# Four layers on 128 small graphs: sums over a graph in any division of the array, s spread as a diagonal, a chunk's sums and its H B⁻¹ Hᵀ in one four-quarter operation

## The chip, the cores and the metric

The kernel runs on one core of a Trainium2 chip. The metric is the device time of one execution in microseconds, the median of three runs. The profile is of one further execution of the same program.

## The reference, cut to what matters

There are 128 graphs of 64 nodes with 512 features each. Four residual layers follow each other, each ending in a layer norm over the features. `A` is the graph's own 64 x 64 matrix `adj`.

```python
# layer 0: additive attention
s = (x @ w) @ a                              # one number per node
A0 = tanh((s_i + s_j) / 8) * 8
A0 = where(A0 >= 0, A0, 0.1 * A0)
A0 = exp(A0) * A;  A0 /= A0.sum(-1);  A0 *= A.sum(-1)
x = layernorm(x + A0 @ x @ w)
# layer 1: attention, adj * exp(q k'), rows divided by their sum
weight = A * exp(q @ k.T);  x = layernorm(x + (weight / weight.sum(-1)) @ v)
# layer 2: a gate, softmax over the nodes of the graph
L = softmax(inv_scale * mask * sum((A @ (k * mask)) * q, -1)) * v
x = layernorm(x + L)
# layer 3: two hypergraph convolutions around a layer norm
H = (A != 0);  D = H @ A[0];  B = H.sum(rows)
conv(h, W) = D^-1 H B^-1 H' (h @ W') + b
x = layernorm(x + conv(layernorm(relu(conv(x, W1))), W2))
```

## The kernel before, in words

Two graphs lie side by side on the 128 partitions: a tile is 64 nodes of one graph on partitions 0 to 63 and 64 of another on 64 to 127. Two tiles make a group (`GT = 2`), so there are 32 groups (`NG`), and two groups make a chunk of four tiles (`CT = 4`), so there are 16 chunks. `run(g)` records all steps of one group, `prepare_chunk(c)` what is computed from `adj` alone for a chunk. The big products with the 512-wide weights are seven-product (Strassen-like) schemes over halves, `seven_products`, which stream their weight pieces (`ring`) from memory. All data are fp32; on TensorE every fp32 product is two passes in the trace (a transpose is one), so a line of the timeline counts twice the products of the code. A 128-row pass with a 128-column load is called whole below.

A product within one graph needs 64 rows and 64 columns of the array only. The kernel marks each TensorE operation with a mode: `whole` (128 x 128), `columns` (128 x 64, in `scores`), or `quarters` (64 x 64). In the quarters mode a product takes a quarter by the partitions of its operands (rows) and of its output (columns). `gathered` uses all four quarters in turn; `over_graph`, the sums and `emit_g` in `prepare_chunk`, and `emit_s` use the two quarters on the diagonal only. In the trace `bank<-kept,x`, `bank<-kept,h` and `bank<-e,x` are `gathered`, `bank<-k,k 128*64` is `scores`, `bank<-e,same` is `over_graph`, `bank<-ident,col 64*64` is `emit_s`, `bank<-ones,adj` and `bank<-w,kept` are the chunk's sums, `bank<-kept,kept` is the chunk's H B⁻¹ Hᵀ, `bank<-ones,e` is layer 1's row sum (f in the code), and `bank<-k,e 64*64` is the product with v after it (po).

Nothing of this is issued as recorded. `Order` is a planner: every operation is added with an engine, an assumed cost, its reads and writes, and a key. `Order.run` then plays the whole program once and takes, on each engine, the ready operation with the lowest key whose buffers are free. On TensorE it charges 145 ns (`TURN`) for a change of mode and prefers an operation of the mode it is in, within `NEAR` (0.5) of the lowest key while in the whole mode and within `FAR` (6.0) otherwise. The order found is pinned on every engine; each engine then issues strictly in it, and everything goes through one recording helper, which is why all lines of the profile carry one line number. Four PSUM banks (kind `bank`) and two pairs (`chx`, `chz`) hold the results of TensorE; `e` is a pool of seven 128 x 2 x 64 buffers.

The parts the change touches, by name: in `prepare_chunk`, `hA` (adj != 0), `be` (one over its row sums), `bh` (hA times be, on GpSimd), `w` (adj's first row with ones beside it), `sums` and `emit_g`; in `run`, `emit_s`, which spreads the column s over the graph, the addition of s to it and the tanh after it; the two uses of `over_graph`, one for layer 0's `e`, one for layer 2's `pr`; and `f`, `ps_f`, `po` of layer 1. Two copies of a chunk's matrix are loaded: `adj` (one transfer) and `turned` (four transfers), in which the tiles' halves are placed so that a four-quarter product meets the right graph.

Of the kernel before, what the change touches and what calls it, by code (L numbers as in the profile page):

```python
# [16 lines left out]
P = 128  # L17
# [37 lines left out]
class Op:  # L55
    __slots__ = ("engine", "cost", "emit", "key", "missing", "users", "takes", "touches", "start", "bytes", "step", "mode", "port", "behind", "group")


class Order:
    LATENCY = {"PE": 220, "DVE": 70, "ACT": 60, "POOL": 60, "SP": 2200}  # L60
    BYTES_PER_NS = 300
    UNDERWAY = 8
    TURN = 145

# [7 lines left out]
    def add(self, engine, cost, reads, writes, emit, urgent=0.0, size=0, mode=None, port=False):  # L72
        o = Op()
        o.engine, o.cost, o.emit, o.key, o.step = engine, cost, emit, self.key - urgent, self.key
        o.start, o.mode, o.port, o.behind, o.group = None, mode, port, None, self.group
        o.users, o.takes, o.touches, o.bytes = [], [], [], size
# [41 lines left out]
    def run(self):  # L118
# [11 lines left out]
        while len(done) < len(self.ops):  # L130
# [4 lines left out]
            for e, heap in ready.items():  # L135
                while free_at[e] <= now:
                    skipped, held, found = [], set(), None
                    while heap:
# [7 lines left out]
                        if item[2].port and port_free > now:  # L146
                            skipped.append(item)
                        elif all(k not in held and len(self.slots[k]) >= c for k, c in need.items()):
                            fits = e != "PE" or item[2].mode == mode
                            if found is None or fits:  # L150
                                if found:
                                    skipped.append(found)
                                found, takes = item, wants
                            else:
                                skipped.append(item)
                            if fits or found[0] < 0:
                                break
                        else:
                            held.update(need)
                            skipped.append(item)  # L160
# [6 lines left out]
                    if e == "PE":  # L167
                        turn, mode = self.TURN if found.mode != mode else 0, found.mode
                    found.start = now
# [60 lines left out]
def kernel(  # L230
# [29 lines left out]
    def sb(name, *shape):  # L260
        return sbuf.tile([P, *shape], FP, name=name)
# [65 lines left out]
    for rows, cols in halves:  # L327
        nc.vector.memset(same[rows, cols], 1.0)

    eye = sb("eye", N)  # L330
    nc.vector.tensor_add(eye, ident[:, :N], ident[:, N:])
# [98 lines left out]
    pe(w_pe(P, KC), [u0], [ps_u0], lambda: emit_u0(ps_u0))  # L430
    act(D, [ps_u0], [u0_b], lambda: nc.scalar.copy(u0_b.t, ps_u0.t))

# [201 lines left out]
    def per_tile(v):  # L634
        return v[:, :, None].to_broadcast([P, CT, N])
# [10 lines left out]
    def prepare_chunk(c):  # L646
        order.key = BASE[GC * c] - 3.0 if c else 0.5
        adj = adjs[c]
        m = mask_c.t[:, ts(c, CT)]
        hA, bh, am = (Buf("kept") for _ in range(3))  # L650
        be = Buf("col")

        dve(W, [adj], [hA, turn], lambda: nc.vector.tensor_scalar(hA.t, adj.t, 0.0, None, ALU.not_equal))
        dve(W, [hA], [be], lambda: nc.vector.tensor_reduce(be.t[:, :CT], hA.t, AX.X, ALU.add))
        dve(CT, [be], [be], lambda: nc.vector.tensor_scalar(be.t[:, :CT], be.t[:, :CT], 1.0, None, ALU.max))
        dve(CT, [be], [be], lambda: nc.vector.reciprocal(be.t[:, :CT], be.t[:, :CT]))

        w = Buf("w")
        act(CT, [adj], [w], lambda: nc.scalar.copy(w.t[:, :, 0:1], adj.t[:, :, 0:1]))

        ps = Buf("bank")

        def sums():
            for left, right, n, at in ((adj, lambda t: ones, 1, 0), (hA, lambda t: w.t[:, t], 2, 1)):
                for t in range(CT):
                    for rows, _ in halves:
                        nc.tensor.matmul(ps.t[rows, 4 * t + at : 4 * t + at + n], left.t[rows, t], right(t)[rows],
                                         start=True, stop=True)

        pe(900, [adj, hA, w], [ps], sums, mode="quarters")  # L670
        radj, n_edges, dn = Buf("col"), Buf("col"), Buf("col")
        g1, dc, dh = Buf("col"), Buf("col"), Buf("col")

        def out(i):
            return ps.t[:, : 4 * CT].rearrange("p (t k) -> p t k", k=4)[:, :, i]

        dve(CT, [ps], [radj], lambda: nc.vector.tensor_copy(radj.t[:, :CT], out(0)), NOW)
        dve(CT, [ps], [dn], lambda: nc.vector.tensor_copy(dn.t[:, :CT], out(1)), NOW)
        dve(CT, [ps], [n_edges], lambda: nc.vector.tensor_copy(n_edges.t[:, :CT], out(2)), NOW)

        dve(CT, [dn], [dc], lambda: nc.vector.tensor_scalar(dc.t[:, :CT], dn.t[:, :CT], TINY, None, ALU.max))
        dve(CT, [dc], [dc], lambda: nc.vector.reciprocal(dc.t[:, :CT], dc.t[:, :CT]))
        dve(CT, [dn, dc], [dc], lambda: nc.vector.scalar_tensor_tensor(
            dc.t[:, :CT], dn.t[:, :CT], 0.0, dc.t[:, :CT], ALU.is_gt, ALU.mult))
        dve(CT, [dc], [dh], lambda: nc.vector.tensor_scalar(dh.t[:, :CT], dc.t[:, :CT], 0.5, None, ALU.mult))

        dve(CT, [dc, n_edges], [g1], lambda: nc.vector.tensor_mul(g1.t[:, :CT], dc.t[:, :CT], n_edges.t[:, :CT]))

        pool(W, [hA, be], [bh], lambda: nc.gpsimd.tensor_mul(bh.t, hA.t, per_tile(be.t[:, :CT])))

        ps_g, gm = Buf("bank"), Buf("kept")

        def emit_g():
            for t in range(CT):
                for rows, _ in halves:
                    nc.tensor.matmul(ps_g.t[rows, ts(t, N)], hA.t[rows, t], bh.t[rows, t], start=True, stop=True)

        pe(500, [hA, bh], [ps_g, gm], emit_g, mode="quarters")
        act(W, [ps_g], [gm], lambda: nc.scalar.copy(flat(gm.t), ps_g.t[:, :W]), NOW)

# [7 lines left out]
        dve(W, [am, mr], [am], lambda: nc.vector.tensor_mul(am.t, am.t, mr.t))  # L708
        prepared[c] = adj, turned_adjs[c], gm, am, radj, g1, dc, dh

# [208 lines left out]
    def over_graph(v, ps):  # L919


        def emit():
            for rows, _ in halves:
                nc.tensor.matmul(ps.t[rows, : GT * N], same[rows, rows], flat(v.t)[rows], start=True, stop=True)

        pe(w_pe(P), [v], [ps], emit, mode="quarters")

# [27 lines left out]
    def run(g):  # L955
# [11 lines left out]

        s = Buf("col", GT)
        for t in range(GT):
            row_dot([xt[[2 * t, 2 * t + 1]], u0_b], s[t], lambda t=t: xt.t[:, t, :], lambda: u0_b.t)  # L970
        ps_s = Buf("bank")

        def emit_s():
            for t in range(GT):
                for rows, cols in halves:
                    nc.tensor.matmul(tiles(ps_s)[rows, t, :], s.t[rows, t : t + 1].to_broadcast([N, N]), ident[rows, cols],
                                     start=True, stop=True)

        pe(300, [s], [ps_s], emit_s, mode="quarters")
        e = Buf("e")  # L980
        dve(GT * N, [ps_s, s], [e], lambda: nc.vector.tensor_add(
            e.t, tiles(ps_s), s.t[:, :GT][:, :, None].to_broadcast([P, GT, N])), NOW)
        act(GT * N, [e], [e], lambda: nc.scalar.activation(e.t, e.t, AF.Tanh, scale=0.125))
        dve(GT * N, [e], [e], lambda: nc.vector.scalar_tensor_tensor(e.t, e.t, 0.1, e.t, ALU.mult, ALU.max))
# [31 lines left out]
        dve(GT * N, [e1, turned], [e1], lambda: nc.vector.tensor_mul(e1.t, e1.t, turned.t[:, own]))  # L1016
        step(6)

        f = Buf("col", GT)
        ps_f = [Buf("bank") for _ in range(GT)]  # L1020

        def quadrants(out, left, right):
            for h, (cols, _) in enumerate(halves):
                for t, (rows, _) in enumerate(halves):
                    nc.tensor.matmul(out(t)[cols], left(h)[rows], right(h)[rows], start=True, stop=True)

        pe(150, [e1], ps_f, lambda: quadrants(lambda t: ps_f[t].t[:, 0:1], lambda h: e1.t[:, h, :], lambda h: ones), mode="quarters")
        po = [Buf("bank") for _ in range(GT)]
        for t in range(GT):
            dve(1, [ps_f[t]], [f[t]], lambda t=t: nc.vector.reciprocal(f.t[:, t : t + 1], ps_f[t].t[:, 0:1]), NOW)  # L1030
        pe(w_pe(D), [e1, v], po, lambda: quadrants(
            lambda t: po[t].t, lambda h: e1.t[:, h, :], lambda h: v.t[:, ts(h, D)]), mode="quarters")
        for t in range(GT):
            dve(D + 40, [po[t], f[t], xt[[2 * t, 2 * t + 1]]], [xt[[2 * t, 2 * t + 1]]],
                lambda t=t: nc.vector.scalar_tensor_tensor(xt.t[:, t, :], po[t].t, f.t[:, t : t + 1], xt.t[:, t, :],
                                                   ALU.mult, ALU.add), NOW)
# [119 lines left out]
    for o in order.run():  # L1156
        for b in o.takes:
            b.t = kinds[b.kind][b.slot]
        if o.behind:
            behind.append(names[o.behind])  # L1160
        o.emit()
        if o.port and o.engine == "DVE":
# [42 lines left out]
```

## Time and profile before

| | |
|---|---|
| median of three runs | 2191.93 us (2191.6 to 2192.64) |
| the profiled execution, its own time | 2194.68 us |
| its span, first to last instruction | 2192.8 us |
| PE busy | 2166.0 us, 21587 passes |
| PEld (weight loads) busy | 1744.5 us |
| DVE busy | 1562.4 us (71%) |
| ACT busy | 823.2 us (38%) |
| POOL busy | 385.7 us (18%) |
| mean granted TensorE clock | 0.997 |
| DMA | 476.44 MB, mean 217 GB/s |

A group of passes in the timeline has a start, a length that reaches to the end of its last pass, and a count. Passes overlap in the array, so what a group costs its engine is the distance from its start to the start of the next group, not its length.

### The profile page before, as it was taken

The page shows a single profiled execution, that of the slowest core. Times are in us where ns is not written, and L with a number is a line of the kernel's source. Part 1 is how long each engine was busy: PE and PEld are TensorE (multiplying, and loading weights), DVE is VectorE, ACT ScalarE, POOL GpSimd, SP SyncE. Part 2 cuts the span into 40 slices and gives each one's busy share as a digit, 9 for nine tenths or more (in the row PEclk, how much of TensorE's full clock was granted, in tenths as well). Part 3 has the DMA queues.
Part 4 walks back from the last instruction along what each step waited for, and adds up shares of the span by engine and source line. Part 5 has one row for each costly group of instructions (what it writes and reads, how often), then busy time and mean ns, then how long its engine had stood idle before and what let it go on. Part 6 is the DMA issues. An engine that isn't in the chain of part 4 may idle for free.

```text
span 2192.8 us, 52900 instructions
## 1 busy us (share of the span) xinstructions
PE 2166.0 (99%) x21587; PEld 1744.5 (80%) x21587; DVE 1562.4 (71%) x4044; ACT 823.2 (38%) x1700; POOL 385.7 (18%) x399
## 2 busy tenths in 40 slices
PE   8999999999999999999999999999999999999998
PEld 4887787888888878888878888788888788888866
DVE  5787766677777777777777777777777777776675
ACT  1344342443334333333433343333343333343433
POOL 1112221121111211112121111211112211122111
PEclk9999999999999999999999999999999999999999
DMA  9766567676665666666576656766556766666475
GB/s 304 255 233 217 192 218 263 202 243 222 211 203 203 207 235 215 209 203 222 197 245 205 210 202 205 228 214 230 197 202 207 240 208 210 203 196 228 154 244 209
DMA packets 174306, 476.44 MB, mean 217 GB/s; under 512 B 35760, under 2 KB 45296, under 8 KB 174064
## 3 DMA queue, kind: packets, MB, share of 16 engines
q1 hardware_dynamic: 174064, 473.05, 64.6%
q8 instruction: 171, 2.80, 0.5%
q14 instruction: 71, 0.58, 0.1%
HBM read 443.33 MB, written 29.66 MB: 216 GB/s over the span
## 4 chain that ended last, share of the span: by engine, by line
PE 97%; DMA 1%; DVE 1%; issue 0%; ACT 0%; SPq 0%; DVEq 0%; ACTq 0%
PE bank L1134 40%; PE chx L1134 35%; PE chz L1134 23%; DMA x<-in_x_dram 0%; DMA out_dram<-x 0%; DMA k<-in_wk_dram 0%; DVE col L1134 0%; DVE x L1134 0%; ACT k L1134 0%; DVE h L1134 0%; ACT x L1134 0%; DVE e L1134 0%; DVE k L1134 0%; SPq L1134 0%; DVE m L1134 0%
## 5 line engine op out<-in xcount | busy, mean ns | idle before, releaser
L1134 PE MATMUL chx<-ring,k 128*128 128x256 f32 (+1 forms) x1664 | 481.2, 418 | 2.6 <-issue 2.0
L1134 PE MATMUL bank<-ring,k 128*128 128x256 f32 (+1 forms) x1536 | 424.5, 417 | 0.3 <-ACT k L1134 0.3
L1134 PEld LDWEIGHTS chx<-ring,k 128*128 128x128 f32 x1664 | 310.2, 191 | 91.7 <-issue 52.7
L1134 POOL TENSOR_TENSOR col<-col,mhalf 128x2 f32<-128x2 f32 (+1 forms) x161 | 111.5, 693 | 1481.1 <-DVE col L1134 910.7
L1134 PEld LDWEIGHTS bank<-ring,k 128*128 128x128 f32 x1536 | 286.2, 191 | 87.4 <-issue 52.0
L1134 ACT COPY k<-bank 128x512 f32<-128x512 f32 (+1 forms) x448 | 226.4, 560 | 343.9 <-PE bank L1134 330.4
L1134 ACT ACTIVATE x<-x,col,col 128x512 f32<-128x512 f32 x256 | 198.2, 811 | 193.1 <-DVE col L1134 185.0
L1134 PE MATMUL chz<-ring,h 128*128 128x256 f32 (+1 forms) x768 | 242.8, 452 | 0.0
L1134 PEld LDWEIGHTS chx<-k,m 128*128 128x128 f32 x1536 | 192.1, 192 | 30.9 <-issue 21.3
L1134 PE MATMUL chx<-k,m 128*128 128x128 f32 x1536 | 203.7, 276 | 0.8 <-DVE h L1134 0.8
L1134 DVE SCALAR_TENSOR_TENSOR x<-chx,col,x 128x256 f32<-128x256 f32 x384 | 173.8, 478 | 42.0 <-PE chx L1134 37.0
L1134 PE MATMUL chz<-ring,k 128*128 128x256 f32 x768 | 201.3, 385 | 0.0
L1134 DVE SCALAR_TENSOR_TENSOR x<-bank,col,x 128x256 f32<-128x256 f32 (+1 forms) x256 | 137.8, 549 | 84.3 <-PE bank L1134 78.7
L1134 PE MATMUL chx<-ring,h 128*128 128x256 f32 (+1 forms) x640 | 181.2, 422 | 0.0
L1134 PEld LDWEIGHTS chz<-ring,h 128*128 128x128 f32 x768 | 141.3, 191 | 48.2 <-issue 34.1
L1134 DVE BATCH_NORM_STATS2 col<-x 128x6 f32<-128x512 f32 x256 | 173.4, 687 | 5.7 <-DVE x L1134 0.5
L1134 PEld LDWEIGHTS chz<-ring,k 128*128 128x128 f32 x768 | 141.9, 191 | 19.6 <-issue 1.4
L1134 PEld LDWEIGHTS chx<-ring,h 128*128 128x128 f32 x640 | 120.6, 191 | 34.5 <-issue 21.0
L1134 DVE SCALAR_TENSOR_TENSOR x<-chz,col,x 128x256 f32<-128x256 f32 x192 | 92.7, 483 | 69.6 <-PE chz L1134 67.1
L1134 ACT ACTIVATE h<-h 128x512 f32<-128x512 f32 x128 | 80.7, 632 | 152.8 <-DVE h L1134 152.3
L1134 PEld LDWEIGHTS chz<-k,m 128*128 128x128 f32 x1024 | 127.0, 192 | 12.3 <-issue 11.9
L1134 PE MATMUL chz<-k,m 128*128 128x128 f32 x1024 | 135.6, 276 | 0.0
(118 smaller groups left out, 2801.5 us busy)
## 6 DMA issues: line engine op xcount, KB each, us to landing
ring<-3a SPq DMA_DIRECT2D x224, 512.0 KB, 4.6
ring<-3b SPq DMA_DIRECT2D x224, 512.0 KB, 4.2
ring<-v SPq DMA_DIRECT2D x189, 512.0 KB, 4.3
ring<-w SPq DMA_DIRECT2D x93, 512.0 KB, 4.5
x<-in_x_dram SPq DMA_DIRECT2D x32, 512.0 KB, 4.5
ring<-v SPq DMA_DIRECT2D x63, 256.0 KB, 3.6
out_dram<-x SPq DMA_DIRECT2D x31, 512.0 KB, 3.3
ring<-w SPq DMA_DIRECT2D x31, 256.0 KB, 4.8
```

Of the source, the lines that this page charges most:

```text
L1134: made = f(*args, **kwargs)
```

## The change

`over_graph` gets the mode `any`: where the planner is in the whole mode the operation is one whole product with the block-diagonal matrix of ones `same`, elsewhere it is two products on the diagonal quarters. The planner decides when it places it. A turn between the two divided modes is now charged at 60 ns, one into or out of the whole mode at 145 ns as before. Layer 0's s is spread by the same `over_graph`: ScalarE multiplies `eye` (two stacked 64 x 64 identities) by s, and the sum over the graph spreads it; the addition of s and the tanh become two activations with a bias, and the factor 1/8 moves into the constant u0. Layer 1's row sums are one whole product of e1 with a two-column matrix `row_of`. The chunk's sums and H B⁻¹ Hᵀ become one operation that reads `turned` and uses all four quarters.

```diff
-    TURN = 145
+    TURN, TURN_DIVIDED = 145, 60
...
-                            fits = e != "PE" or item[2].mode == mode
+                            fits = e != "PE" or item[2].mode in (mode, "any")
...
-                        turn, mode = self.TURN if found.mode != mode else 0, found.mode
+                        if found.mode == "any":
+                            found.mode = "whole" if mode in ("whole", None) else "quarters"
+                            found.args = (found.mode == "whole",)
+                        if found.mode != mode:
+                            turn = self.TURN if "whole" in (found.mode, mode) else self.TURN_DIVIDED
+                        mode = found.mode
...
+    row_of = sb("row_of", GT)
+    nc.vector.memset(row_of, 0.0)
+    for t, (rows, _) in enumerate(halves):
+        nc.vector.memset(row_of[rows, t : t + 1], 1.0)
...
-    act(D, [ps_u0], [u0_b], lambda: nc.scalar.copy(u0_b.t, ps_u0.t))
+    act(D, [ps_u0], [u0_b], lambda: nc.scalar.activation(u0_b.t, ps_u0.t, AF.Identity, scale=0.125))
...
-        dve(W, [adj], [hA, turn], lambda: nc.vector.tensor_scalar(hA.t, adj.t, 0.0, None, ALU.not_equal))
+        dve(W, [turned], [hA, turn], lambda: nc.vector.tensor_scalar(hA.t, turned.t, 0.0, None, ALU.not_equal))
...
-        pe(900, [adj, hA, w], [ps], sums, mode="quarters")
...
-        pe(500, [hA, bh], [ps_g, gm], emit_g, mode="quarters")
-        act(W, [ps_g], [gm], lambda: nc.scalar.copy(flat(gm.t), ps_g.t[:, :W]), NOW)
...
+        ps = [Buf("bank") for _ in range(2)]
+        def quarters_of(n, at, left, right):
+            for g in range(CT // 2):
+                for h, (cols, _) in enumerate(halves):
+                    for t, (rows, _) in enumerate(halves):
+                        nc.tensor.matmul(ps[t].t[cols, at(g) : at(g) + n], left.t[rows, 2 * g + h], right(2 * g + h)[rows],
                                          start=True, stop=True)
+        def emit_g():
+            quarters_of(N, lambda g: N * g, hA, lambda i: bh.t[:, i])
+            quarters_of(1, lambda g: P + 3 * g, turned, lambda i: ones)
+            quarters_of(2, lambda g: P + 3 * g + 1, hA, lambda i: w.t[:, i])
+        pe(720, [turned, hA, bh, w], [*ps, gm], emit_g, mode="quarters")
+        for t in range(2):
+            act(P, [ps[t]], [gm], lambda t=t: nc.scalar.copy(
+                gm.t.rearrange("p (g t) i -> p t g i", t=2)[:, t], ps[t].t[:, :P].rearrange("p (g i) -> p g i", i=N)), NOW)
+            dve(6, [ps[t]], [sums], lambda t=t: nc.vector.tensor_copy(
+                sums.t[:, : 3 * CT].rearrange("p (k g t) -> p t g k", t=2, k=3)[:, t],
+                ps[t].t[:, P : P + 6].rearrange("p (g k) -> p g k", k=3)), NOW)
...
-        def emit():
-            for rows, _ in halves:
+        def emit(whole):
+            for rows in (slice(0, P),) if whole else (rows for rows, _ in halves):
                 nc.tensor.matmul(ps.t[rows, : GT * N], same[rows, rows], flat(v.t)[rows], start=True, stop=True)
-        pe(w_pe(P), [v], [ps], emit, mode="quarters")
+        pe(w_pe(P), [v], [ps], emit, mode="any")
...
-        pe(300, [s], [ps_s], emit_s, mode="quarters")
-        dve(GT * N, [ps_s, s], [e], lambda: nc.vector.tensor_add(
-            e.t, tiles(ps_s), s.t[:, :GT][:, :, None].to_broadcast([P, GT, N])), NOW)
-        act(GT * N, [e], [e], lambda: nc.scalar.activation(e.t, e.t, AF.Tanh, scale=0.125))
+            act(N + 40, [s[t]], [diag[t]], lambda t=t: nc.scalar.activation(diag.t[:, t], eye, AF.Identity, scale=s.t[:, t : t + 1]))
+        over_graph(diag, ps_s)
+        for t in range(GT):
+            act(N + 40, [ps_s, s[t]], [e[t]], lambda t=t: nc.scalar.activation(
+                e.t[:, t], tiles(ps_s)[:, t], AF.Tanh, bias=s.t[:, t : t + 1]), NOW)
...
-        pe(150, [e1], ps_f, lambda: quadrants(lambda t: ps_f[t].t[:, 0:1], lambda h: e1.t[:, h, :], lambda h: ones), mode="quarters")
+        pe(110, [e1], [ps_f], lambda: nc.tensor.matmul(ps_f.t[:, :GT], flat(e1.t), row_of, start=True, stop=True))
+        dve(GT, [ps_f], [f], lambda: nc.vector.reciprocal(f.t[:, :GT], ps_f.t[:, :GT]), NOW)
```

More of the change, by code (lines that the diff above doesn't have):

```diff
@@ L55 @@
 class Op:
-    __slots__ = ("engine", "cost", "emit", "key", "missing", "users", "takes", "touches", "start", "bytes", "step", "mode", "port", "behind", "group")
+    __slots__ = ("engine", "cost", "emit", "key", "missing", "users", "takes", "touches", "start", "bytes", "step", "mode", "port", "behind", "group", "args")
 class Order:
@@ L74, in add @@
         o.engine, o.cost, o.emit, o.key, o.step = engine, cost, emit, self.key - urgent, self.key
-        o.start, o.mode, o.port, o.behind, o.group = None, mode, port, None, self.group
+        o.start, o.mode, o.port, o.behind, o.group, o.args = None, mode, port, None, self.group, ()
         o.users, o.takes, o.touches, o.bytes = [], [], [], size
@@ L647, in prepare_chunk @@
         order.key = BASE[GC * c] - 3.0 if c else 0.5
-        adj = adjs[c]
+        adj, turned = adjs[c], turned_adjs[c]
         m = mask_c.t[:, ts(c, CT)]
@@ L656, in prepare_chunk @@
         dve(CT, [be], [be], lambda: nc.vector.reciprocal(be.t[:, :CT], be.t[:, :CT]))
+        pool(W, [hA, be], [bh], lambda: nc.gpsimd.tensor_mul(bh.t, hA.t, per_tile(be.t[:, :CT])))
         w = Buf("w")
[L659 to L665, printed above, removed]
-                    for rows, _ in halves:
-                        nc.tensor.matmul(ps.t[rows, 4 * t + at : 4 * t + at + n], left.t[rows, t], right(t)[rows],
-                                         start=True, stop=True)
@@ L670, in prepare_chunk @@
-        pe(900, [adj, hA, w], [ps], sums, mode="quarters")
-        radj, n_edges, dn = Buf("col"), Buf("col"), Buf("col")
-        g1, dc, dh = Buf("col"), Buf("col"), Buf("col")
[L674 to L679, printed above, removed]
@@ L681, in prepare_chunk @@
-        dve(CT, [dn], [dc], lambda: nc.vector.tensor_scalar(dc.t[:, :CT], dn.t[:, :CT], TINY, None, ALU.max))
+        act(CT, [turned], [w], lambda: nc.scalar.copy(w.t[:, :, 0:1], turned.t[:, :, 0:1]))
+        ps = [Buf("bank") for _ in range(2)]
+        gm, sums = Buf("kept"), Buf("col")
+        def quarters_of(n, at, left, right):
[3 more added lines that the diff above has]
+                        nc.tensor.matmul(ps[t].t[cols, at(g) : at(g) + n], left.t[rows, 2 * g + h], right(2 * g + h)[rows],
+                                         start=True, stop=True)
@@ L682, in prepare_chunk @@
+        radj = sums
+        dn, n_edges = (slice(CT * k, CT * (k + 1)) for k in (1, 2))
+        g1, dc, dh = Buf("col"), Buf("col"), Buf("col")
+        dve(CT, [sums], [dc], lambda: nc.vector.tensor_scalar(dc.t[:, :CT], sums.t[:, dn], TINY, None, ALU.max))
         dve(CT, [dc], [dc], lambda: nc.vector.reciprocal(dc.t[:, :CT], dc.t[:, :CT]))
-        dve(CT, [dn, dc], [dc], lambda: nc.vector.scalar_tensor_tensor(
-            dc.t[:, :CT], dn.t[:, :CT], 0.0, dc.t[:, :CT], ALU.is_gt, ALU.mult))
+        dve(CT, [sums, dc], [dc], lambda: nc.vector.scalar_tensor_tensor(
+            dc.t[:, :CT], sums.t[:, dn], 0.0, dc.t[:, :CT], ALU.is_gt, ALU.mult))
@@ L685, in prepare_chunk @@
         dve(CT, [dc], [dh], lambda: nc.vector.tensor_scalar(dh.t[:, :CT], dc.t[:, :CT], 0.5, None, ALU.mult))
[L687 to L696, printed above, removed]
@@ L698, in prepare_chunk @@
-        pe(500, [hA, bh], [ps_g, gm], emit_g, mode="quarters")
-        act(W, [ps_g], [gm], lambda: nc.scalar.copy(flat(gm.t), ps_g.t[:, :W]), NOW)
+        dve(CT, [dc, sums], [g1], lambda: nc.vector.tensor_mul(g1.t[:, :CT], dc.t[:, :CT], sums.t[:, n_edges]))
         order.key += 6.0
@@ L708, in prepare_chunk @@
         dve(W, [am, mr], [am], lambda: nc.vector.tensor_mul(am.t, am.t, mr.t))
-        prepared[c] = adj, turned_adjs[c], gm, am, radj, g1, dc, dh
+        prepared[c] = adj, turned, gm, am, radj, g1, dc, dh
     KEYS = ("11", "12", "21", "22")
@@ L919, in over_graph @@
     def over_graph(v, ps):
-        def emit():
-            for rows, _ in halves:
+        def emit(whole):
+            for rows in (slice(0, P),) if whole else (rows for rows, _ in halves):
                 nc.tensor.matmul(ps.t[rows, : GT * N], same[rows, rows], flat(v.t)[rows], start=True, stop=True)
-        pe(w_pe(P), [v], [ps], emit, mode="quarters")
+        pe(w_pe(P), [v], [ps], emit, mode="any")
     def z_into(zT, bias=None):
@@ L968, in run @@
         s = Buf("col", GT)
+        diag, e, ps_s = Buf("e", GT), Buf("e", GT), Buf("bank")
         for t in range(GT):
             row_dot([xt[[2 * t, 2 * t + 1]], u0_b], s[t], lambda t=t: xt.t[:, t, :], lambda: u0_b.t)
[L971 to L977, printed above, removed]
-        pe(300, [s], [ps_s], emit_s, mode="quarters")
-        e = Buf("e")
-        dve(GT * N, [ps_s, s], [e], lambda: nc.vector.tensor_add(
-            e.t, tiles(ps_s), s.t[:, :GT][:, :, None].to_broadcast([P, GT, N])), NOW)
-        act(GT * N, [e], [e], lambda: nc.scalar.activation(e.t, e.t, AF.Tanh, scale=0.125))
+            act(N + 40, [s[t]], [diag[t]], lambda t=t: nc.scalar.activation(diag.t[:, t], eye, AF.Identity, scale=s.t[:, t : t + 1]))
[3 more added lines that the diff above has]
+                e.t[:, t], tiles(ps_s)[:, t], AF.Tanh, bias=s.t[:, t : t + 1]), NOW)
         dve(GT * N, [e], [e], lambda: nc.vector.scalar_tensor_tensor(e.t, e.t, 0.1, e.t, ALU.mult, ALU.max))
@@ L1017, in run, with emit_po @@
         step(6)
-        f = Buf("col", GT)
-        ps_f = [Buf("bank") for _ in range(GT)]
-        def quadrants(out, left, right):
+        f = Buf("col")
+        ps_f = Buf("bank")
+        pe(110, [e1], [ps_f], lambda: nc.tensor.matmul(ps_f.t[:, :GT], flat(e1.t), row_of, start=True, stop=True))
+        dve(GT, [ps_f], [f], lambda: nc.vector.reciprocal(f.t[:, :GT], ps_f.t[:, :GT]), NOW)
+        po = [Buf("bank") for _ in range(GT)]
+        def emit_po():
             for h, (cols, _) in enumerate(halves):
                 for t, (rows, _) in enumerate(halves):
-                    nc.tensor.matmul(out(t)[cols], left(h)[rows], right(h)[rows], start=True, stop=True)
-        pe(150, [e1], ps_f, lambda: quadrants(lambda t: ps_f[t].t[:, 0:1], lambda h: e1.t[:, h, :], lambda h: ones), mode="quarters")
-        po = [Buf("bank") for _ in range(GT)]
+                    nc.tensor.matmul(po[t].t[cols], e1.t[rows, h, :], v.t[rows, ts(h, D)], start=True, stop=True)
+        pe(w_pe(D), [e1, v], po, emit_po, mode="quarters")
         for t in range(GT):
[L1030 to L1034, printed above, removed]
+            dve(D + 40, [po[t], f, xt[[2 * t, 2 * t + 1]]], [xt[[2 * t, 2 * t + 1]]],
                 lambda t=t: nc.vector.scalar_tensor_tensor(xt.t[:, t, :], po[t].t, f.t[:, t : t + 1], xt.t[:, t, :],
@@ L1160 @@
             behind.append(names[o.behind])
-        o.emit()
+        o.emit(*o.args)
         if o.port and o.engine == "DVE":
```

## The prediction

> **What bounds the kernel now.** I read the page's busy row first, then the chain that ended last.
>
> ```profile
> PE 2166.0 (99%) x21587; PEld 1744.5 (80%) x21587; DVE 1562.4 (71%) x4044; ACT 823.2 (38%) x1700; POOL 385.7 (18%) x399
> PE 97%; DMA 1%; DVE 1%; issue 0%; ACT 0%; SPq 0%; DVEq 0%; ACTq 0%
> ```
>
> TensorE is busy for 99% of the span and is 97% of the chain. Next, the waits of TensorE alone (us in total, times, longest):
>
> ```profile
> PE bank L1134 <- DMA k<-in_wk_dram: 6.3, 1, 6.3
> PE bank L1134 <- issue: 6.1, 4, 2.9
> PE bank L1134 <- DVE e L1134: 3.7, 2, 2.0
> PE chx L1134 <- issue: 2.0, 3, 1.2
> ```
>
> All eight rows of that view (four small ones are not shown) come to 19.6 us, of which 10.0 lie in the first 80 us. So no other engine's work is on the path in the steady state, and the change is worth what it takes from or adds to TensorE's own time. A busy share of 99% does not say that this time is product time, because overlapping passes and turns of the array are inside it. The timeline shows that. The distance between the starts is the cost of a line:
>
> ```profile
> 1018.71 1.06 PE L1134 MATMUL chx<-k,m 128*128 128x128 f32 x8
> 1019.70 1.15 PE L1134 MATMUL bank<-k,k 128*64 128x64 f32 x32
> 1020.78 1.13 PE L1134 MATMUL chx<-ring,k 128*128 128x256 f32 x4
> 1021.75 1.05 PE L1134 MATMUL bank<-k,m 128*128 128x128 f32 x8
> ```
>
> Eight `k,m` passes cost 0.89 us where a whole operation follows (1024.37 to 1025.26), and 0.99 here; four `ring` passes cost 0.86 (1022.64 to 1023.50), and 0.97 here. That is 0.10 us on the way into a divided mode and 0.11 on the way back. The third part is the exit from the divided block:
>
> ```profile
> 1053.93 1.16 PE L1134 MATMUL bank<-kept,x 64*64 64x64 f32 x64
> 1054.91 0.40 PE L1134 MATMUL bank<-e,same 64*64 64x128 f32 x4
> 1055.14 0.59 PE L1134 MATMUL bank<-ones,adj 64*64 64x1 f32 x16
> 1055.57 0.62 PE L1134 MATMUL bank<-w,kept 64*64 64x2 f32 x16
> 1056.04 0.68 PE L1134 MATMUL bank<-kept,kept 64*64 64x64 f32 x16
> 1056.53 0.41 PE L1134 MATMUL bank<-ident,col 64*64 64x64 f32 x8
> 1056.88 1.98 PE L1134 MATMUL chx<-ring,k 128*128 128x512 f32 x4
> ```
>
> Three prices are read here. `kept,x` uses four quarters: 64 passes in 0.98 us, 0.0153 each. The chunk's sums and `kept,kept` use two: 16 passes in 0.43, 0.47 and 0.49 us, 0.029 each. The eight `ident,col` should cost 8 x 0.029 = 0.23 us and cost 0.35, so the exit is 0.12. One trip from the whole mode into a divided one and back is 0.10 + 0.12 + 0.11 = 0.33 us. A change between the two divided modes costs the exit once: 32 `k,k` passes take 1.08 us ahead of quarters as well (1038.99 to 1040.07), so I take 0.13.
>
> **The change part by part.** How often the modes turn is read from the order of TensorE's instructions in the two built programs; counting is not timing.
>
> Turns. Before there are 168 trips between whole and divided (55 enter with `scores`, 113 with quarters); after there are 117 (57 and 60). Turns between columns and quarters go from 40 to 56. So -51 x 0.33 = -16.8 us, and 16 x 0.13 = +2.1. Much of this comes from the planner grouping otherwise: blocks such as po, then `gathered`, now stand side by side. 13 + 10 of the old blocks were `kept,x`, `e,same` and then `ident,col`, which were joined already; the lone ones went.
>
> Chunk operation. Before: 0.43 + 0.47 + 0.49 = 1.39 us per chunk. After: the same 48 passes over four quarters, 48 x 0.0153 = 0.73. Times 16: -10.5 us. [...] Two of the four quarters share their rows[...]. The `kept,x` row is just this arrangement and runs at half the cost per pass, so I take the row[...].
>
> Spreading s. `emit_s` goes: 8 passes x 0.029 = 0.23 us, times 32 = -7.4. One more `over_graph` comes per group. Four `e,same` passes cost 0.23 us here and 0.22 elsewhere (722.65 to 722.87); as one whole product it is two passes of 128 columns at 0.89/8 = 0.111, again 0.22. So mode `any` saves turns and no passes. 96 instead of 64 of them (by the order 76 in quarters, 20 whole) is 32 x 0.225 = +7.2.
>
> Layer 1's row sums. Before, eight passes in quarters, 25 times directly behind po:
>
> ```profile
> 1044.88 1.09 PE L1134 MATMUL bank<-k,e 64*64 64x512 f32 x8
> 1045.79 0.24 PE L1134 MATMUL bank<-ones,e 64*64 64x1 f32 x8
> 1045.97 1.13 PE L1134 MATMUL chx<-ring,k 128*128 128x256 f32 x4
> ```
>
> po with them costs 1.09 us; without (358.18 to 359.20) 1.02. So they cost 0.07, and the seven that stood alone some 8 x 0.015 = 0.12 beside their counted trip: 25 x 0.07 + 7 x 0.12 = 2.6 us. After, two whole passes with two columns. [...] The trace has a nearer row: eight whole passes `ones,k` with one column take 33.12 to 34.10, less 0.10 for the way into quarters, 0.11 each, as long as 128 columns. So 32 x 0.22 = +7.0[...], and this step costs +4.4 by the row[...].
>
> Other engines. DVE loses 32 additions of 268 ns, 32 reciprocals of 166 ns and 16 of 48 copies. ACT gains 64 spreading activations, which like `e<-bank,col` 128x64 I put at 312 ns (20 us); 64 of 312 for 32 of 308 in the tanh (+10); and two copies near 277 for one of 373 per chunk (+3). ACT goes from 38% to about 40% busy, under a TensorE that is full: nothing, as long as TensorE has other ready groups. If that cover fails, the wait is the second rival. The scaled u0 and the setting of `row_of` come once, beside the first loads, for which TensorE waits 6.3 us anyway. POOL has the same `bh` (612 ns). SP issues no transfer more; the chunk's operation now needs the four `turned` transfers (4.1 us to landing) instead of the one `adj`, and all of `bh`, `w` and `hA` before its first pass, with every later product queued behind it. The planner asks for it a good step ahead of its first user, so 0 in the steady state, up to 1 us for a chunk at the start. It takes two PSUM banks of four at once: between 0 and, if each of the 16 stood a copy (0.37 us) longer, +6; taken 0, as it replaces two operations with a bank each.
>
> Start. Two stretches (us from:to, length, then busy of PE, PEld, DVE, ACT, POOL, clock, DMA share):
>
> ```profile
> 50.00:60.00 10.00, 6.32 (x116) 4.83 (x116) 8.36 (x24) 3.59 (x7) 2.34 (x4) 0.83 0.95 329
> 60.00:70.00 10.00, 10.00 (x56) 8.70 (x55) 4.43 (x14) 2.44 (x8) 2.17 (x2) 0.66 0.41 130
> ```
>
> Around two waits for `e` (1.96 and 1.71 us) the granted clock falls; at half clock that is 3.4 + 6.8 us, half of which, 5.1, is lost. In the new order group 1's sum of `e` stands directly ahead of its `gathered`, so a wait of that kind is still there (reciprocal 0.95, product 0.32). DMA is full in the first 60 us. I count the start unchanged, and give back 0.8 us for the first two chunks, whose saved product time is then waited for.
>
> Sum: -16.8 + 2.1 - 10.5 - 7.4 + 7.2 + 4.4 + 0.8 = -20.2 us. The profiled execution (span 2192.8, own time 2194.68) is 2.75 us above the median of the runs; carried to the median, 2191.93 - 20.2 = 2171.7, so **2172 us**, -0.9%.
>
> **Rivals.**
> First, the sum holds: 0.70. Its own range is 2163 to 2180 (price of a trip 0.28 to 0.38, 2.5 each way; new waits or none after 80 us, where there were 9.6).
> Second, slower: the operation that spreads s now waits for ACT, which waits for DVE's row dots, where before it waited for DVE alone; the tanh follows on ACT. TensorE is in order, so if ACT reaches these late behind 811 ns normalizations, every product behind stands. One such 0.8 us activation in front of each of the two steps in each group is 32 x 1.6 = 51 us at most, giving 2223; it decides from 20.2/32 = 0.63 us per group. Against it: ACT is 62% idle and TensorE waited for ACT 0.5 us in all. 0.07.
> Third, the gain is half: the quarters give nothing [...] or joining blocks only turns a trip into a change of mode at nearly full price (16 x 0.2 = 3). 2172 + 10.5 + 3 = 2185. [...]against it: the rows. 0.10.
> Fourth, more: the start has no half clock and part of the 8.1 us of "issue" goes. 2172 - 9 = 2163 and down to 2157. For it: group 1's layer 0 stands earlier in the new order. 0.13.
> That the change does not do what it says is excluded for the turns by the order, and left for the quarters in the third.
>
> **How the numbers follow.** A difference of 0.2% (4.4 us) is about what a measurement of this kernel can tell. First and fourth are faster (0.83); of the third 0.08 is faster and 0.02 within; of the second 0.01 faster, 0.01 within, 0.05 slower. Together 0.92, 0.03, 0.05. The range goes from the fourth to the third, 2158 to 2186, and leaves out the second and the tails.
>
> **What would show it.** Right: `kept,kept`, `ones,adj` and `w,kept` at 0.015 us per pass start to start; `row_of,e` at 0.22 us per pair; PE's waits still near 20 us; the trips unchanged at 0.33. Wrong: waits of PE for ACT `e` of 20 us or more (second); the chunk's lines still near 1.4 us (third); a time below 2158 without a change in waits, which would mean that a trip costs more than 0.38.

## The result, and the profile after

The changed kernel takes 2175.99 us (2175.15 to 2176.97, four runs) where the kernel before took 2192.28 us in the same session (2191.60 to 2193.03). The ratio is 0.9926 with an interval of 0.9909 to 0.9943: 16.3 us less. The profiled executions lie 19.4 us apart in span (2192.8 and 2173.4); the one of before was 2.4 us over its median and the one after 0.8 under its own, which is the rest.

The page's busy row and chain of after:

```profile
PE 2144.7 (99%) x21227; PEld 1727.1 (79%) x21227; DVE 1534.2 (71%) x3967; ACT 854.6 (39%) x1812; POOL 384.2 (18%) x399
PE 98%; issue 0%; ACT 0%; DVE 0%; DMA 0%; SPq 0%; DVEq 0%; ACTq 0%
```

TensorE is still the bound. It issues 360 passes fewer, and its busy time falls by 21.3 us. The passes alone, at the prediction's prices, account for 6.3 of that (-10.5 - 7.4 + 7.2 + 4.4). The other 15.0 is close to the 14.7 counted for turns, so turns of the array had been counted as busy. ACT carries 31 us more, which brings it from 38% to 39%. All waits of TensorE after the change (us in total, times, longest; "issue" is time in which it waited for nothing that the profile shows):

```profile
PE bank L1133 <- issue: 8.5, 7, 3.1
PE bank L1133 <- DMA k<-in_wk_dram: 6.1, 1, 6.1
PE bank L1133 <- DVE e L1133: 3.4, 2, 2.2
PE bank L1133 <- ACT k L1133: 1.5, 3, 0.7
PE chx L1133 <- ACT k L1133: 1.4, 2, 1.2
PE bank L1133 <- ACT u_b L1133: 0.7, 1, 0.7
```

They sum to 21.6 us against 19.6. The row that was feared, ACT `e`, is not there; ACT `k`, the copies out of PSUM, rose from 0.5 to 2.9. The two waits for DVE `e` at the start are as before.

The timeline of one chunk of after, inside a divided block (start, length, passes):

```profile
1008.36 1.06 PE L1133 MATMUL chx<-k,m 128*128 128x128 f32 x8
1009.35 1.15 PE L1133 MATMUL bank<-k,k 128*64 128x64 f32 x32
1010.43 0.33 PE L1133 MATMUL bank<-e,same 64*64 64x128 f32 x2
...
1011.37 0.41 PE L1133 MATMUL bank<-e,same 64*64 64x128 f32 x4
1011.72 1.13 PE L1133 MATMUL chx<-ring,k 128*128 128x256 f32 x4
1012.68 1.05 PE L1133 MATMUL bank<-k,m 128*128 128x128 f32 x8
```

Between the two `e,same` lines stand the chunk's 48 passes. Everything from 1009.35 to 1011.72, four operations of three kinds, now shares one trip: the way in is 0.10 us (0.99 for eight `k,m`) and the way back 0.10 (0.96 for four `ring`), the prices of before.

### The profile page after: what moved, and what is told of

It reads as the page before. It is cut to its first block, busy times and chain, and to the rows that moved or that the text cites. A ratio compares the mean times of both kernels' runs of the same rounds, so it can differ in the third digit from the quotient of the medians.

```text
span 2173.4 us, 52324 instructions
## 1 busy us (share of the span) xinstructions
PE 2144.7 (99%) x21227; PEld 1727.1 (79%) x21227; DVE 1534.2 (71%) x3967; ACT 854.6 (39%) x1812; POOL 384.2 (18%) x399
## 4 chain that ended last, share of the span: by engine, by line
PE 98%; issue 0%; ACT 0%; DVE 0%; DMA 0%; SPq 0%; DVEq 0%; ACTq 0%
PE bank L1133 40%; PE chx L1133 35%; PE chz L1133 23%; ACT k L1133 0%; DMA k<-in_wk_dram 0%; ACT x L1133 0%; DVE col L1133 0%; DVE x L1133 0%; DVE e L1133 0%; ACT u_b L1133 0%; ACT bw_b L1133 0%; SPq L1133 0%; DVEq L1133 0%; ACTq L1133 0%
## 5 line engine op out<-in xcount | busy, mean ns | idle before, releaser
L1133 PEld LDWEIGHTS chz<-ring,k 128*128 128x128 f32 x768 | 140.6, 191 | 21.5 <-issue 2.4
```

The lines of the kernel that those rows point to most:

```text
L1133: made = f(*args, **kwargs)
```

## The experiments

The main theory is the prediction's: TensorE's time is a sum of passes and turns by count. Its rivals are that turns are cheap, that quarters don't run side by side, and, since the changed kernel showed a 3.1 us wait on issue inside its longest block, that quick passes outrun the supply of instructions. Each ratio is to the kernel before, run on the same chip; its median was 2192.28, 2194.28, 2193.44 and 2193.52 us in the four sessions, so the ratios are to be compared and not the times. A trip is one passage from the whole mode into a divided one and back, a switch is a change between columns and quarters; both are counted in the order of TensorE's instructions.

| run | us | ratio (interval) | trips, switches | waits on issue, us |
|---|---|---|---|---|
| before | 2192.28 | 1 | 168, 40 | 8.1 |
| after | 2175.99 | 0.9926 (0.9909 to 0.9943) | 117, 56 | 8.5 |
| two_quarters | 2184.37 | 0.9949 (0.9934 to 0.9963) | 117, 56 | 7.1 |
| before_near1 | 2276.58 | 1.0371 (1.0356 to 1.0387) | 138, 38 | 13.0 |
| after_near0 | 2180.55 | 0.9933 (0.9918 to 0.9948) | 159, 44 | 2.4 |
| quarters_always | 2190.27 | 0.9984 (0.9973 to 0.9996) | 152, 45 | 12.1 |
| any_only | 2204.16 | 1.0049 (1.0031 to 1.0067) | 140, 55 | 16.7 |
| chunk_only | 2201.10 | 1.0033 (1.0021 to 1.0045) | 178, 38 | 9.5 |
| capped_near1 | 2185.60 | 0.9964 (0.9952 to 0.9977) | 105, 34 | 10.5 |
| shift_half | 2173.44 | 0.9911 (0.9896 to 0.9925) | 117, 56 | 5.9 |
| f_twice | 2181.87 | 0.9943 (0.9925 to 0.9960) | 117, 56 | 8.5 |
| tuned | 2176.00 | 0.9915 (0.9899 to 0.9931) | 113, 44 | 2.1 |
| any_only_shift | 2217.02 | 1.0098 (1.0077 to 1.0118) | 140, 55 | 21.6 |
| before_shift | 2206.69 | 1.0056 (1.0039 to 1.0072) | 168, 40 | 14.1 |

**Do four quarters run side by side?** two_quarters:

```diff
-                for h, (cols, _) in enumerate(halves):
+                for h in range(2):
...
-                        nc.tensor.matmul(ps[t].t[cols, at(g) : at(g) + n], left.t[rows, 2 * g + h], right(2 * g + h)[rows],
+                        nc.tensor.matmul(ps[h].t[rows, at(g) : at(g) + n], left.t[rows, 2 * g + h], right(2 * g + h)[rows],
```

> The changed kernel with the chunk's 24 products on the two diagonal quarters instead of four; order, counts and turns on TensorE are the same (117 trips, 56 switches). The chunk's results land on other partitions and are not those of the reference. Theory (the passes of four quarters run side by side, 0.0153 us each against 0.029): 48 passes x 0.0137 x 16 chunks = +10.5 us against the changed kernel's 2176, so about 2186.5, and the chunk's lines back at 1.4 us. Rival (two quarters that share their rows run one after the other, and the gain of the change comes from turns alone): 2176, no change.

The same block in its timeline:

```profile
1014.78 0.44 PE L1133 MATMUL bank<-e,same 64*64 64x128 f32 x4
1015.05 0.63 PE L1133 MATMUL bank<-kept,kept 64*64 64x64 f32 x16
1015.51 0.58 PE L1133 MATMUL bank<-ones,adj 64*64 64x1 f32 x16
1015.95 0.61 PE L1133 MATMUL bank<-w,kept 64*64 64x2 f32 x16
1016.42 0.41 PE L1133 MATMUL bank<-e,same 64*64 64x128 f32 x4
1016.76 1.13 PE L1133 MATMUL chx<-ring,k 128*128 128x256 f32 x4
```

From the first `e,same` to `ring` it is 1.98 us, and 1.29 with four quarters (1010.43 to 1011.72): 0.69 per chunk, 11.0 for 16. The spans differ by 8.9; its waits are 1.3 us shorter and its mean granted clock is 0.997 for 0.996. The 11.0, less these 1.3 and an estimate of 2.2 for the clock (0.001 of the span), leave 7.5. The prediction read the two prices from `kept,x` (0.0153 us a pass over four quarters) and from the chunk's old lines (0.029 over two), which make 0.66 per chunk; this run shows 0.69 for the chunk itself.

**What is a trip worth, with the products unchanged?** before_near1 and after_near0 change the planner's preference alone; quarters_always takes the mode `any` back out of the changed kernel.

```diff
# before_near1
-    NEAR, FAR = 0.5, 6.0
+    NEAR, FAR = 1.0, 3.0
# after_near0
-    NEAR, FAR = 0.5, 6.0
+    NEAR, FAR = 0, 6.0
# quarters_always
...
-        pe(w_pe(P), [v], [ps], emit, mode="any")
+        pe(w_pe(P), [v], [ps], emit, mode="quarters")
```

> The kernel before with NEAR, FAR = 1.0, 3.0 and nothing else: the same products in another order, 138 trips between whole and divided modes instead of 168, 38 switches between columns and quarters instead of 40. Theory (a trip costs 0.33 us): 30 x 0.33 + 2 x 0.13 = -10.2, about 2182. Rival (turns are cheap or hidden, what the change saved are passes): 2192, within 2 us.

> The changed kernel with NEAR = 0: the same products, 159 trips instead of 117 and 44 switches instead of 56, and no divided block above 160 passes (the changed kernel has two above 200). Theory (price of a trip alone): 42 x 0.33 - 12 x 0.13 = +12.3, about 2188. Rival one (turns are cheap): 2176. Rival two (long divided blocks stall on the supply of instructions, so that shorter blocks get back the part of the 8.5 us of issue waits that lies in them): 2188 less 3 to 6, about 2183.

> The changed kernel with the sums over a graph always in quarters: 152 trips instead of 117, 45 switches instead of 56, and nine divided blocks of 228 passes each. Theory (price of a trip alone): 35 x 0.33 - 11 x 0.13 = +10.1, about 2186. Rival (supply of instructions: quick passes use them up faster than they arrive, so each block of over 200 passes stalls 2 to 3 us as the one of 240 did in the changed kernel): 9 x 2 to 9 x 3 more, 2204 to 2213, with the waits on issue in the lines of the 64 x 64 passes.

before_near1 fell far outside every expectation. It has 30 trips fewer and is 82 us slower. The first rows of its waits:

```profile
PE chz L1134 <- DVE h L1134: 19.4, 12, 1.7
PE bank L1134 <- issue: 13.0, 8, 2.8
PE bank L1134 <- DVE col L1134: 10.0, 23, 0.8
PE bank L1134 <- DVE x L1134: 7.1, 23, 0.3
```

All its rows come to 78.7 us against 19.6, of which 50.8 against 4.7 are for VectorE. This order put products ahead of the evictions and sums that feed them, so TensorE waited for VectorE; counting turns does not see that. The 59.1 us of added waits and an estimate of 13.6 at half clock (a mean of 0.991 for 0.997), less the 10.2 by count, make 62.5 of the 82; what the other 20 are stays open. So this run says nothing on the price of a trip.

after_near0 has 42 trips more than the changed kernel and in span only 4.8 us more. By count it should be +12.3; its waits are 14.9 us for 21.6 and its clock 0.997 for 0.996 (an estimate of 2.2 us less at half clock), which leaves 3.4. Were turns free, the same sum would be -8.9. So the trips cost about what they should, and shorter waits, 2.4 us on issue for 8.5, won most of it back. quarters_always is the reverse: +10.1 by count, +2.6 of waits, an estimate of +2.2 of clock (0.995 for 0.996) make 14.9, and its span is 13.7 longer; with free turns it would be 4.8. Its nine blocks of 228 passes did not all wait, as the rival had it; four waits of 2.0 to 2.6 us stood in them.

**The parts alone.**

```diff
# any_only: the kernel before, with
-        pe(w_pe(P), [v], [ps], emit, mode="quarters")
+        pe(w_pe(P), [v], [ps], emit, mode="any")
# and TURN, TURN_DIVIDED = 145, 60, as in the change
...
# chunk_only: the kernel before, with
-        pe(900, [adj, hA, w], [ps], sums, mode="quarters")
...
-        pe(500, [hA, bh], [ps_g, gm], emit_g, mode="quarters")
+        pe(720, [turned, hA, bh, w], [*ps, gm], emit_g, mode="quarters")
```

> The kernel before with the mode any for the sums over a graph and the price of 60 ns for a turn between divided modes, and nothing else: same products, 140 trips instead of 168, 55 switches instead of 40. Theory (0.33 per trip, 0.13 per switch): -9.2 + 2.0 = -7.2 us against before, a ratio of 0.9967. Rival (supply of instructions takes it back where blocks join): between 0 and -4, and the waits on issue above the 8.1 us of before.

> The kernel before with the new chunk operation alone: 178 trips instead of 168, 38 switches instead of 40. Theory: 16 chunks from 1.39 to 0.70 us is -11.1, plus 10 x 0.33 - 2 x 0.13 = +3.0 for turns, -8.1 us against before, a ratio of 0.9963. Rival (the passes of the quarters do not run side by side where blocks are short, as the time of the run with two quarters, 5 to 8 us above the changed kernel where 10.5 was expected, might mean): -3 or less.

Both are slower than before. The waits on issue of any_only, then of chunk_only those and ACT's:

```profile
PE bank L1139 <- issue: 13.5, 7, 3.4
...
PE chz L1139 <- issue: 1.6, 1, 1.6
PE chx L1139 <- issue: 1.6, 2, 1.3
```

```profile
PE bank L1131 <- issue: 9.5, 5, 3.0
...
PE bank L1131 <- ACT k L1131: 5.0, 17, 1.0
```

any_only: -7.2 by count, +10.7 of waits (30.3 for 19.6), an estimate of +2.2 of clock (0.996 for 0.997); the sum is +5.7 and its span 6.8 longer. chunk_only: -8.1 by count and +8.8 of waits; its span is 3.8 longer, 3 of which I can't place. By these sums the parts save about what was counted, and their orders lose more in waits.

**Why TensorE waits on issue.** In the trace I counted all of TensorE's records (passes, loads and the few others) in order of time up to each gap. In the changed kernel the wait at 430.2 us stands at record 8129, those at 341.3, 767.5 and 1294.3 at 6337, 15041 and 25793; in the kernel before those at 348.7 and 574.2 at 6593 and 11201. Each number leaves 193 when divided by 256. In the profiles of these fourteen kernels 105 gaps of over 0.15 us between 80 and 2150 us stand at this remainder. All 98 waits on issue in that stretch are among them, and none stands elsewhere; the other seven are put down to ACT or VectorE. The page counts 168 transfers on the queue "instruction" and 2 x 21227 passes and loads, 253 per transfer. The view of that queue between 430.8 and 431.0 us of the changed kernel has one, and none in the 3.8 us ahead of it or the 3.3 behind:

```profile
q8 instruction: 1, 0.02, 29.4%
```

The wait ends at 433.3, 2.4 us later. In the other gaps that lag is 2.2 to 2.6 us mostly, 4.2 at most. In quarters 256 records, 128 passes with their loads, last 128 x 0.0153 = 1.96 us; with whole passes of 256 columns (eight `ring` in 1.73 us, 0.216 each) they last 28. The stretches around this wait (from:to, length, busy of PE, PEld, DVE, ACT, POOL, clock, DMA share):

```profile
427.00:429.90 2.90, 2.90 (x170) 2.77 (x166) 2.42 (x12) 1.53 (x6) 0.00 (x0) 1.00 1.03 378
429.90:433.20 3.30, 0.30 (x20) 0.16 (x8) 2.19 (x9) 0.78 (x2) 0.00 (x0) 1.00 0.99 344
433.20:436.00 2.80, 2.69 (x29) 1.08 (x29) 0.69 (x1) 1.28 (x3) 0.05 (x1) 0.51 0.26 72
```

336 records in 2.9 us, then nothing, while the DMA share is 0.99. The pause costs twice, for the granted clock then stands at 0.50 for 3.4 us (433.2 to 436.6). That is not so for every pause: of 25 waits of 2.4 us or more at this remainder, 18 were followed by a stretch of half clock and 7 were not, the 2.9 us at 348.7 of the kernel before among them (1.00 over the 2.4 us behind it).

Quick passes alone seldom make these waits. The transfer above began some 0.7 us after TensorE had stopped, so it was late itself. In the fourteen profiles 177 boundaries follow 256 records that were used up in under 4 us. Where the DMA share of the 4 us ahead was 0.75 or more, 81 of 127 had such a gap, on average 1.05 us over all 127; below that it was 10 of 50, and 0.12 us. So the gaps go with a busy DMA as well, but no run changed its load alone, and why a transfer begins late stays open.

To test whether the place of the boundary makes the waits, all later instructions were shifted by 128, half of 256 (64 passes with their loads), in the same order:

```diff
+    for i in range(32):
+        rows = halves[i % 2][0]
+        nc.tensor.matmul(kinds["bank"][3][rows, 0:1], same[rows, rows], ones[rows], start=True, stop=True)
     eye = sb("eye", N)
```

> The changed kernel with 32 small quarter products (128 instructions with their loads) at TensorE's start, while it waits for the first weights: everything after stands 128 instructions later in TensorE's stream, half of one instruction transfer, and in the same order. Theory (supply): the waits on issue move to other blocks and their sum changes by some us (changed kernel: 3.1 us at 430, 1.4 at 1888, 1.3 at 1294), each still ending 2 to 3 us after the start of an instruction transfer; time 2176 +- 5. Rival (something in these blocks themselves, banks or semaphores): the same blocks wait as long as before.

> The kernel before with the mode any alone (which ran 0.5% slower than before, with 16.7 us of waits on issue), and 32 small quarter products at TensorE's start as in the run shift_half: same order, all later instructions 128 further in the stream. Theory (supply: which blocks wait depends on where the transfers' boundaries fall): its waits on issue change by 4 us or more and the time with them. Rival (they belong to the blocks): they stay at 16.7 within 1 us, in the same places, and the ratio stays at 1.005.

> The kernel before with the same 32 small quarter products at TensorE's start. Control for the shift: theory (supply): the waits on issue (8.1 us) move to other blocks, and time changes by what their sum changes, within 5 us either way. Rival (the added products gain or lose something at the start itself, such as the clock, and that is what the run shift_half showed): the same 2 to 3 us as there, with the waits on issue in their old places.

The waits moved. In shift_half the block of the 3.1 us wait has none on issue (`kept,h`, 64 passes at 429.96 in 1.11 us), a new one of 2.4 us stands at 1957, and the sum is 5.9 for 8.5; the ratio, 0.9911, is not clear of 0.9926. The shift of the kernel before lost: 14.1 us on issue for 8.1, and a span 12.9 longer.

```profile
PE bank L1138 <- issue: 12.0, 8, 2.8
...
PE chx L1138 <- issue: 2.1, 3, 0.9
```

The same shift of any_only took its waits from 16.7 to 21.6. So one shift shortens the waits of one kernel and lengthens those of two: which blocks wait depends on where the boundary falls. Nor do the added products slow the start: at 109 us the same pass stands 1.7 us earlier in the shifted kernel than in the kernel before, and the loss comes later in steps, the largest of 4.8 us across the new wait of 2.8 us at 511.6. The control went beyond the 5 us that I gave it: all waits 25.5 for 19.6 and a clock of 0.995 for 0.997 explain an estimate of 10.3 of the 12.9.

**The pair of two-column passes.** f_twice:

```diff
-        pe(110, [e1], [ps_f], lambda: nc.tensor.matmul(ps_f.t[:, :GT], flat(e1.t), row_of, start=True, stop=True))
+        pe(110, [e1], [ps_f], lambda: [nc.tensor.matmul(ps_f.t[:, :GT], flat(e1.t), row_of, start=True, stop=True) for _ in range(2)])
```

> The changed kernel with layer 1's row sums computed twice over (the same whole product issued a second time into the same bank), in the same order with the same turns. Theory by the changed kernel's own timeline (a pair of row_of passes costs 0.14 us start to start there): +32 x 0.14 = +4.5, ratio to before up by 0.002. Rival, as the prediction had it (a pass of two columns costs as much as one of 128, 0.22 a pair): +7.0, ratio up by 0.0032. The 128 added instructions also move the boundaries of the instruction transfers, which can add or take some 4 us; so the pair's own lines decide.

In the changed kernel, then in f_twice:

```profile
1032.51 0.28 PE L1133 MATMUL bank<-row_of,e 128*128 128x2 f32 x2
1032.65 1.97 PE L1133 MATMUL chx<-ring,k 128*128 128x256 f32 x8
1034.55 1.09 PE L1133 MATMUL bank<-k,e 64*64 64x512 f32 x8
```

```profile
1031.40 0.50 PE L1133 MATMUL bank<-row_of,e 128*128 128x2 f32 x4
1031.77 1.97 PE L1133 MATMUL chx<-ring,k 128*128 128x256 f32 x8
1033.67 1.09 PE L1133 MATMUL bank<-k,e 64*64 64x512 f32 x8
```

The second pair takes 0.37 - 0.14 = 0.23 us. The 0.14 of the first was misleading: the eight `ring` behind it cost 1.90, where they cost 1.73 and 0.10 for the way into quarters, so 0.07 of it lies there. My expectation of 0.14 fell; the prediction's 0.22 holds. The time alone would have misled: the span is 4.3 us longer, as 32 x 0.14 would have it, but its clock is 0.998 for 0.996, an estimate of 4 us less at half clock, against 32 x 0.23 = 7.4.

**A better order?** Both are the changed kernel with other preferences and a cap on a divided block.

```diff
-    NEAR, FAR = 0.5, 6.0
+    NEAR, FAR = 0.75, 4.0     # tuned; capped_near1: 1.0, 3.0 and TURN, TURN_DIVIDED = 165, 130
+    CAP = 3600                # tuned; capped_near1: 3200
...
-                            fits = e != "PE" or item[2].mode in (mode, "any")
+                            fits = e != "PE" or item[2].mode in ("whole" if quick + item[2].cost > self.CAP else mode, "any")
...
+                        quick = 0 if mode == "whole" else quick + found.cost
```

> The changed kernel with NEAR, FAR = 1.0, 3.0, turns charged at 165 and 130, and a cap on the planned cost of a divided block (3200 ns): 105 trips instead of 117, 34 switches instead of 56, no block above 176 passes. Theory (turns by count, and the supply of instructions keeps up in shorter blocks): -4.0 - 2.9 - 7 to -10, so 14 to 17 us under the changed kernel, about 2160. Rival (an order with NEAR = 1 runs the groups out of step, so that TensorE waits for VectorE, as in the kernel before with NEAR = 1, which lost 82 us): above 2190, with waits for DVE of 20 us and more.

> The changed kernel with NEAR, FAR = 0.75, 4.0 and a cap of 3600 ns on the planned cost of a divided block: 113 trips instead of 117, 44 switches instead of 56, no block above 164 passes, ten above 150 (changed kernel: 15, two above 200). Theory (turns by count, issue waits only in long blocks): -1.3 - 1.6 - 4 to -7, so 7 to 10 us under the changed kernel, ratio 0.988 to 0.9895. Rival (another order brings other waits, for ACT or DVE, or other blocks onto the boundaries of the transfers): at or above the changed kernel's 0.9926.

capped_near1 has the fewest trips of all and loses to the changed kernel, which is the rival's side, though the waits are on ACT (12.7 us) and issue (10.5) and not on DVE. tuned has 1.9 and 0.2 us on issue and still ends at 0.9915, not clear of the changed kernel: its waits for ACT `k` and DVE `x` are 4.7 and 2.2 us where they were 2.9 and none, and its span is only 0.7 us shorter. No version clearly beats it.

## Why the prediction was right, point by point

- **The bound.** Right: TensorE at 99%, and the other engines' changed work is invisible.
- **Turns** (-16.8 and +2.1). The counts are exact and the price of a trip is the same in the lines of after. after_near0 and quarters_always agree with it to 1.4 us once their waits and an estimate for the clock are added.
- **Chunk** (-10.5). 0.69 us per chunk instead of 0.66: -11.0.
- **Spread of s** (-7.4 and +7.2). No run took it alone. What the trace shows is that a spread in quarters costs 0.35 us with its exit (1011.37 to 1011.72), as `ident,col` did.
- **Row sums** (+4.4). 0.21 and 0.23 per pair for 0.22; `ones,k`, the row that the prediction took, was the right one.
- **Start** (+0.8). Not to be separated; its two waits for `e` are there (3.4 us for 3.7), with a granted clock of 0.55 from 50 to 60 us and 0.94 from 60 to 70.
- **Waits** (counted at nothing, with a margin). This is the mis-sized term: +2.0 us on the list, most of it ACT `k`, and an estimate of 2.1 us more at half clock from the clocks of 0.997 and 0.996. Sum by measured prices: -16.8 + 2.1 - 11.0 - 0.2 + 4.4 = -21.5, with the waits and the clock -17.4, in span -19.4. The prediction's 2172 was 4 us low against the medians. That a new order would bring so few new waits was argued for ACT alone, and the rest was luck: the same count gave the wrong sign for any_only, chunk_only and before_near1, whose waits rose by 10.7, 8.8 and 59.1 us.
- **Second rival** (TensorE waits for ACT's spread of s). Did not occur. In other orders, though, waits of its size did, for VectorE's `h` and `col` and for instructions. The range was right for this order; it would not have held for a neighbouring one.

## What to carry to other kernels

When TensorE is full, count its mode trips and price them from a place where a short block stands between long products; a trip of 0.33 us was worth more than eight quarter passes (0.12 us over four quarters, 0.23 over two). But an order that is better by count is a new order: its waits have to be measured, and a part that loses alone may still belong in the whole. Before an order is called better by half a per cent, shift its instructions by 128 and measure again: the kernel before, so shifted, was 0.56% slower in the same order.

## What the runs showed of the hardware that was not expected

- Runs of quick passes stood still where another 256 records of TensorE had been used up, mostly while the DMA was busy (81 of 127 boundaries at a DMA share of 0.75 or more, 10 of 50 below). The gaps stand at one remainder of 256 (193), last up to 4.0 us (capped_near1), and end 2.2 to 2.6 us after an instruction transfer starts in most cases. 128 added instructions at the start made the same program 0.56% slower (before_shift).
- After a wait of 3.1 us the granted clock was 0.51 over the next 2.8 us, and a stretch of half clock followed in 18 of 25 waits of 2.4 us or more.
- The distance between starts hid part of the pair of two-column passes in the line behind it: 0.14 us shown, 0.21 to 0.23 paid.
